# Graph layer with one-hot matmuls: two of the ten edge-against-slot comparison rows of a set made on ScalarE instead of VectorE

## The chip, the cores and the metric

The kernel runs on one core of a Trainium2 chip. The metric is the device time of one launch in microseconds. The time given for a kernel is the median of several runs; the profile shows one execution, whose own time is given beside its span.

## The reference

A graph has N = 6250 nodes with D = 64 features and E = 206250 edges, sorted by destination. What is computed is

```python
h   = relu(layernorm(x))                                # (6250, 64), no gain, no shift
msg = relu(h[src] + edge_attr)                          # (206250, 64)
agg = segment_sum(msg, dst, num_segments=6250)
out = x + relu((h + agg) @ W1 + b1) @ W2 + b2           # (6250, 64)
```

`dst` is sorted in ascending order; `src` is in no order, so `h[src]` is a gather.

## The kernel before, in words

**Groups and sets.** Edges are handled in groups of 1024 (128 partitions by 8 columns): 201 full groups and a short one at the end. Two groups, an even and an odd one, make a set `k`. Sets 2 to 99 take part in the scheme that the change touches: 98 sets.

**Two ways of fetching `h[src]`.** Of the 16 columns of a set, 10 are fetched by indirect DMAs on GpSimd's queue (`gather`, L160, one instruction for one column). The other 6 columns (4 of the even group and 2 of the odd one, `T = 6`) are fetched by TensorE with one-hot matrices, in three steps:

- Each edge of the six columns was given, in a ranking stage at the beginning, one of 128 slots in one of `SB = 10` parts of the nodes. For each set, `source` (L346) brings the node number of every slot into a row in DRAM and back, spread over all partitions. `find` (L365) compares that row with node numbers on VectorE, which gives `found`, and `slots_of` (L381) multiplies `found` with the table `hp` of h (three bf16 pieces that add up to the float32 value). The result is a PSUM tile `rows`, which ScalarE copies into the SBUF tile `picked` (`slots_out`, L393, L394). This is done for two parts at a time: 5 products of 10 matmuls and 5 copies for each set.
- `spot` (L359) loads a row of numbers that says in which part and slot each of the set's 768 edges lies, spread over all partitions. `back` (L373) compares this row with `ids`, the numbers 4096 + 128 m + partition, for each part m: ten comparisons of 768 elements for each set, 16-bit integers in and bf16 ones and zeros out. Their result is the one-hot matrix `backs`, slots by edges.
- `pick` (L406) multiplies `backs` with `picked`, ten matmuls for each of the six columns, into PSUM tiles `pick`. VectorE adds up the three pieces and the edge's attributes (L466).

**Messages and sums.** `messages` (L459) adds the gathered columns (L464, VectorE), reduces the `pick` tiles (L466, VectorE), and makes the ReLU on ScalarE (L469). `window_sum` (L472) sums messages into 48 destinations by matmuls with a one-hot matrix (L478). `take` (L450, L456) and `room` (L396, L403) copy edge attributes into PSUM on ScalarE ahead of time. Every 16 or 17 groups a finished block of 512 nodes goes through the two matrix products (`hidden`, `result`, `store`).

**Order.** The order of work is written out by hand: each engine works through its instructions in the order in which the Python code emits them. `half(g)` (L526) emits one group's part. For a set in the steady state the orders of the two engines that matter are:

- TensorE, even half: rows of parts 0 and 1; `source` products (L351); `window_sum` of the group before; rows of parts 2 and 3; `pick` of the odd group (20 matmuls). Odd half: rows of parts 4 and 5, of 6 and 7, of 8 and 9; `window_sum`; `pick` of the next even group (40 matmuls).
- ScalarE, even half: the `source` copy (L353); `picked` of parts 0 and 1; ReLU; `take`; `room`; `picked` of parts 2 and 3. Here `back` is called, after `pick`. Odd half: `picked` of parts 4 and 5, of 6 and 7; ReLU; `take`; `picked` of parts 8 and 9; `room` (two copies).

The PSUM tile `rows` has two buffers, used in turn by all of `slots_of` and `source`. So a product of `slots_of` can begin only when the tile two before it has been copied out by ScalarE:

```python
ps = psum.tile([P, 2, 3 * D], F32, name="rows", bufs=2)      # slots_of, L383
ps = psum.tile([SB, P], F32, name="rows", bufs=2)            # source, L349
```

`backs` and `spots` have two buffers each. Gathered columns have nine (`LOOK`), so GpSimd's gathers can run up to nine groups ahead of the messages.

Of the kernel before, what the change touches and what calls it, by code (L numbers as in the profile page):

```python
# [9 lines left out]
F32 = mybir.dt.float32  # L10
# [4 lines left out]
AF = mybir.ActivationFunctionType  # L15
# [5 lines left out]
P = 128  # L21
# [23 lines left out]
SB, BB, BN = 10, 5, 125  # L45
KB = SB * BB
PART = BB * BN
EVEN, ODD = 4, 2
T = EVEN + ODD
K0, K1 = 2, NG // 2  # L50
KS = K1 - K0
ROUND = 1.5 * 2 ** 23
# [8 lines left out]
def kernel(  # L61
# [14 lines left out]
    nc = tc.nc  # L76
    ctx.enter_context(tc.manual_schedule())

    const = ctx.enter_context(tc.tile_pool(name="const", bufs=1))
# [27 lines left out]
    for t_sb, tail in ((src_sb, src_tail), (dst_sb, dst_tail)):  # L107
# [18 lines left out]
    ones = const.tile([P, P], F32, name="ones")  # L126
# [11 lines left out]
    ids = const.tile([P, SB], F32, name="ids")  # L138
    nc.gpsimd.iota(ids, pattern=[[P, SB]], base=BIAS, channel_multiplier=1,
                   allow_small_or_imprecise_dtypes=True)  # L140
    hp = const.tile([P, KB, 3, D], BF16, name="hp")
    nc.vector.memset(hp[:, KB - 1], 0.0)

# [80 lines left out]

    part = const.tile([P, KS, T], BF16, name="part")
    node = const.tile([P, KS, T], F16, name="node")
    nodes_of = const.tile([P, BB], F32, name="nodes_of")
    nc.gpsimd.iota(nodes_of, pattern=[[P, BB]], base=1, channel_multiplier=1, allow_small_or_imprecise_dtypes=True)
    place = const.tile([P, KS, T], F32, name="place")
    spot_rows = dram.tile([KS * T, P], BF16, name="spot_rows")  # L230
    of_part = const.tile([P, SB], BF16, name="of_part")
    nc.gpsimd.iota(of_part, pattern=[[1, SB]], base=0, channel_multiplier=0, allow_small_or_imprecise_dtypes=True)
    fits = const.tile([P, KS, T], F32, name="fits")

    def of_sets(t_sb, even):
        v = t_sb[:, K0 * 2 * G:K1 * 2 * G].rearrange("p (k j) -> p k j", j=2 * G)
        return v[:, :, G - EVEN:G] if even else v[:, :, 2 * G - ODD:]
# [6 lines left out]
    def ranks(pool):  # L244
        src_f = pool.tile([P, KS, T], F32, name="src_f")
        nc.vector.tensor_copy(src_f[:, :, :EVEN], of_sets(src_sb, True))
# [81 lines left out]
    holds, masks, backs, sources, spots, found, picked, halves = {}, {}, {}, {}, {}, {}, {}, {}  # L328
# [44 lines left out]
    def back(k):  # L373

        row = spots.pop(k).bitcast(I16)
        backs[k] = hot.tile([P, SB, T, P], BF16, name="backs")
        for m in range(SB):
            nc.vector.tensor_scalar(backs[k][:, m].rearrange("p t s -> p (t s)"), row, ids[:, m:m + 1], None,  # L378
                                    op0=ALU.is_equal)

    def slots_of(k, m, n):  # L381

        ps = psum.tile([P, 2, 3 * D], F32, name="rows", bufs=2)  # L383
        for i in range(n):
            for b in range(BB):
                nc.tensor.matmul(ps[:, i], found[k][:BN, b, m + i, :],  # L386
                                 hp[:BN, (m + i) * BB + b].rearrange("p t d -> p (t d)"),
                                 start=(b == 0), stop=(b == BB - 1))
        if m == 0:
            picked[k] = hot.tile([P, SB, 3 * D], BF16, name="picked")  # L390
        halves[k, m] = ps[:, :n]
# [134 lines left out]
    def half(g, groups=True, sets=True):  # L526
# [36 lines left out]
        if even:  # L563
            if now:
                back(k + 1)
            if sets and is_set(k + 3):
                mask(k + 3)
        elif sets:
            if is_set(k + 2):
                find(k + 2)  # L570
            if is_set(k + 3):
                hold(k + 3)
# [43 lines left out]
    with tc.tile_pool(name="nodes", bufs=2) as nodes:  # L616

        for k, n in ((0, KB // 2), (KB // 2, KB - 1 - KB // 2), (KB - 1, 1)):
            p = min(BN, N - k * BN)
# [111 lines left out]
```

## Time and profile before

| | |
|---|---|
| time, median of 3 runs | 1386.8 us (1383.34 to 1388.13) |
| the profiled execution's own time | 1385.12 us |
| its span | 1383.3 us |
| mean granted TensorE clock | 0.964 of full speed |
| busy: TensorE matmul / weight load | 1242.3 us (90%) / 1163.1 us (84%) |
| busy: VectorE | 1185.2 us (86%) |
| busy: ScalarE | 508.4 us (37%) |
| busy: GpSimd | 1022.5 us (74%) |
| the ten comparisons of `back`, L378 | 980 instructions, 335.5 us, mean 415 ns |
| gathers, L160 (from `h_rows`) | 992 instructions, 987.2 us, mean 995 ns |

The span is the time from the first to the last instruction of the profiled execution. Engine shares are averages over the whole span. PE is TensorE's matmuls, PEld its weight loads, DVE is VectorE, ACT ScalarE, POOL GpSimd, and SP the engine that issues most DMAs. A line of the timeline gives the start in microseconds, the busy time, the engine, the line of the kernel, the operation with its output and input, the number of instructions merged into it, and in brackets the idle time before it and what ended it. Instructions of one engine can overlap by a tenth of a microsecond in the records.

### The profile page before, as it was taken

Reading aid. Unit: us, or ns where it says so; the run is one execution under the profiler, and the core shown is the slowest. Engines: PE = TensorE matmul, PEld = TensorE weight load, DVE = VectorE, ACT = ScalarE, POOL = GpSimd, SP = SyncE. Lnnn points to the kernel's source line nnn. Section 1 sums busy time; section 2 is a strip of 40 time slices with the busy share of each in tenths; the row PEclk is TensorE's granted clock in tenths of the full one; section 3 lists DMA queues with packets and bytes.
Section 4 is the critical chain, followed back from the end, with each engine's and each line's share of the span. In section 5 each row is a group of like instructions: output and inputs, shape, how many; then the busy total and the mean of one; then the engine's idle time right before and its main releaser. Section 6 shows DMA issues by size and latency. Waiting matters only on the chain.

```text
span 1383.3 us, 37550 instructions
## 1 busy us (share of the span) xinstructions
PE 1242.3 (90%) x14894; PEld 1163.1 (84%) x14894; DVE 1185.2 (86%) x2847; ACT 508.4 (37%) x1356; POOL 1022.5 (74%) x1035
## 2 busy tenths in 40 slices
PE   1624899999999999999999999999999999989994
PEld 0413799999999999999999999999998998988983
DVE  6765999899899899999898899898998998888972
ACT  2321333433343333443433433334333443333331
POOL 7672777777777777777777777777777777777774
PEclk9766999999999999999999999999999999999996
DMA  5331434434444444444444444444444443443431
GB/s 169 92 71 55 116 86 119 120 100 114 126 118 112 104 116 122 122 117 106 112 117 122 122 108 110 114 119 117 107 112 119 122 118 96 118 119 92 121 75 25
DMA packets 107766, 150.42 MB, mean 109 GB/s; under 512 B 33857, under 2 KB 52673, under 8 KB 107585
## 3 DMA queue, kind: packets, MB, share of 16 engines
q1 hardware_dynamic: 73569, 112.65, 27.5%
q0 software_dynamic: 32768, 33.62, 12.5%
q8 instruction: 118, 1.93, 0.6%
q10 hardware_dynamic: 1248, 1.70, 0.4%
q14 instruction: 63, 0.52, 0.1%
HBM read 144.27 MB, written 3.60 MB: 107 GB/s over the span
## 4 chain that ended last, share of the span: by engine, by line
PE 61%; DMA 8%; POOL 8%; DVE 6%; issue 5%; ACT 2%; DVEq 0%; POOLq 0%; SPq 0%; ACTq 0%
PE pick L412 27%; PE rows L386 21%; PE agg L478 10%; POOL xg L160 8%; DMA xg<-h_rows,src_sb 5%; PE rows L351 2%; DVE backs L378 2%; DVE full L466 1%; DVE found L370 1%; DMA sources<-source_row 1%; PE rows L499 1%; ACT picked L394 1%; PE rows L486 1%; DMA spots<-spot_rows 1%; ACT full L456 1%
## 5 line engine op out<-in xcount | busy, mean ns | idle before, releaser
L160 POOL DMA_INDIRECT xg<-h_rows,src_sb x992 | 987.2, 995 | 334.4 <-issue 264.3
L412 PE MATMUL pick<-picked,backs 128*128 128x192 bf16 x5880 | 517.1, 246 | 23.5 <-ACT pick L403 20.7
L412 PEld LDWEIGHTS <-backs 128*128 128x128 bf16 x5880 | 488.9, 98 | 28.2 <-issue 21.4
L386 PE MATMUL rows<-hp,found 125*128 125x192 bf16 x4900 | 459.8, 247 | 6.5 <-DVE found L370 5.7
L386 PEld LDWEIGHTS <-found 125*128 125x128 bf16 x4900 | 404.8, 98 | 18.3 <-DVE found L370 7.4
L378 DVE TENSOR_SCALAR backs<-spots,ids 128x768 bf16<-128x768 int16 x980 | 335.5, 415 | 0.0
L394 ACT CAST picked<-rows 128x384 bf16<-128x384 f32 x490 | 234.3, 478 | 274.2 <-PE rows L386 269.4
L370 DVE TENSOR_SCALAR found<-sources,nodes_of 125x1280 bf16<-125x1280 int16 x490 | 251.0, 577 | 38.0 <-DMA sources<-source_row 37.6
L466 DVE TENSOR_REDUCE full<-pick 128x128 f32<-128x512 f32 x294 | 205.7, 700 | 67.5 <-PE pick L412 36.0
L478 PEld LDWEIGHTS agg<-oh,msg 128*64 128x64 f32 x3224 | 205.7, 139 | 37.2 <-issue 19.4
L478 PE MATMUL agg<-oh,msg 128*64 128x48 f32 x3224 | 231.0, 226 | 4.3 <-ACT msg L469 4.3
L353 ACT CAST source<-rows 10x128 int16<-10x128 f32 x98 | 25.0, 255 | 456.4 <-PE rows L351 451.8
L469 ACT ACTIVATE msg<-full 128x512 f32<-128x512 f32 x202 | 119.5, 592 | 49.0 <-DVE full L466 26.8
L464 DVE TENSOR_TENSOR full<-full,xg 128x256 f32<-128x256 f32 (+1 forms) x202 | 99.1, 491 | 33.4 <-DMA xg<-h_rows,src_sb 22.8
L440 DVE TENSOR_TENSOR oh<-slot,wslots 128x384 f32<-128x384 int16 x202 | 109.9, 544 | 0.0
L333 DVE TENSOR_TENSOR holds<-place,wslots 128x768 f16<-128x768 f32 x98 | 92.4, 943 | 6.0 <-DMA spot_rows<-sp 6.0
L456 ACT COPY full<-ea 128x256 f32<-128x256 f32 (+1 forms) x202 | 87.2, 432 | 0.0
L403 ACT COPY pick<-ea 128x128 f32<-128x128 f32 x294 | 72.0, 275 | 0.0
L351 PE MATMUL rows<-holds,mask 128*10 128x128 f16 x588 | 49.6, 221 | 4.6 <-DVE mask L343 4.6
L351 PEld LDWEIGHTS <-mask 128*10 128x10 f16 x588 | 31.5, 88 | 21.7 <-issue 19.9
L435 DVE TENSOR_TENSOR z<-z,agg 64x48 f32 x202 | 38.2, 189 | 6.4 <-PE agg L478 3.3
L160 POOL DMA_INDIRECT xg<-in_x_dram,src_sb x32 | 33.4, 1044 | 10.9 <-issue 9.4
(101 smaller groups left out, 284.4 us busy)
## 6 DMA issues: line engine op xcount, KB each, us to landing
ea<-in_edge_attr_dram SPq DMA_DIRECT2D x201, 256.0 KB
sources<-source_row SPq DMA_DIRECT2D x98, 320.0 KB
spots<-spot_rows SPq DMA_DIRECT2D x98, 192.0 KB
xg<-h_rows,src_sb POOLq DMA_INDIRECT x992
source_row<-source SPq DMA_DIRECT2D x98, 2.5 KB
x_sb<-in_x_dram SPq DMA_DIRECT2D x4, 384.0 KB
h_rows<-ln_h SPq DMA_DIRECT2D x4, 384.0 KB
xb<-in_x_dram SPq DMA_DIRECT2D x12, 128.0 KB
```

Source lines behind the costliest of these rows:

```text
L160: nc.gpsimd.indirect_dma_start(out=xg[:, j, :], out_offset=None, in_=rows[:, :], in_offset=bass.IndirectOffsetOnAxis(ap=idx[:, j:j + 1], a ...
L351: nc.tensor.matmul(ps, mk[:, t, :], oh[:, t, :], start=(t == 0), stop=(t == T - 1))
L370: nc.vector.tensor_scalar(found[k][:BN, b].rearrange("p m s -> p (m s)"), row[:BN], nodes_of[:BN, b:b + 1], None, op0=ALU.is_equal)
L378: nc.vector.tensor_scalar(backs[k][:, m].rearrange("p t s -> p (t s)"), row, ids[:, m:m + 1], None, op0=ALU.is_equal)
L386: nc.tensor.matmul(ps[:, i], found[k][:BN, b, m + i, :], hp[:BN, (m + i) * BB + b].rearrange("p t d -> p (t d)"), start=(b == 0), stop=(b ...
L394: nc.scalar.copy(picked[k][:, m:m + n], halves.pop((k, m)))
L412: nc.tensor.matmul(pk[:, u, :3].rearrange("p t d -> p (t d)"), backs[k][:, m, t0 + i + u, :], picked[k][:, m], start=(m == 0), stop=(m == ...
L440: nc.vector.tensor_tensor(oh[:, :n], slot[:, cols_of(g)].unsqueeze(2).to_broadcast([P, n, W]), wslots[:, :W].unsqueeze(1).to_broadcast([P, ...
L456: nc.scalar.copy(full[:, :n], taken[g][2][:, :n])
L466: nc.vector.tensor_reduce(full[:, m + i:m + i + c], pk[:, :c].rearrange("p j t d -> p j d t"), AX.X, ALU.add)
L469: nc.scalar.activation(msg[:, :n], full[:, :n], AF.Relu)
L478: nc.tensor.matmul(pa, msg[:, j, :], oh[:, j, :], start=(j == 0), stop=(j == n - 1))
```

## The change

A constant `ids_neg` is made once, the negative of `ids`. In `back`, VectorE makes the comparisons for parts 0 to 7. For parts 8 and 9 ScalarE makes two activations each: the absolute value of the edge's number less the slot's number, written as bf16, and then in place the ReLU of one less that distance, which is 1 where the numbers agree and 0 elsewhere. ScalarE's instructions are emitted where `back` is called, that is behind the copy of `picked` for parts 2 and 3.

```diff
+SA = 2
...
+    ids_neg = const.tile([P, SB], F32, name="ids_neg")
+    nc.vector.tensor_scalar_mul(ids_neg, ids, -1.0)
...
         row = spots.pop(k).bitcast(I16)
         backs[k] = hot.tile([P, SB, T, P], BF16, name="backs")
-        for m in range(SB):
+        for m in range(SB - SA):
             nc.vector.tensor_scalar(backs[k][:, m].rearrange("p t s -> p (t s)"), row, ids[:, m:m + 1], None,
                                     op0=ALU.is_equal)
+        for m in range(SB - SA, SB):
+            at = backs[k][:, m].rearrange("p t s -> p (t s)")
+            nc.scalar.activation(at, row, AF.Abs, bias=ids_neg[:, m:m + 1])
+            nc.scalar.activation(at, at, AF.Relu, bias=ones[:, 0:1], scale=-1.0)
```

## The prediction, made before the changed kernel was run

> **What bounds the kernel now.** I read the page's busy shares and its chain first, then the timeline of TensorE and of ScalarE over one set, then the groups by shape for durations, and the waits.
>
> ```profile
> PE 1242.3 (90%) x14894; PEld 1163.1 (84%) x14894; DVE 1185.2 (86%) x2847; ACT 508.4 (37%) x1356; POOL 1022.5 (74%) x1035
> ...
> PE 61%; DMA 8%; POOL 8%; DVE 6%; issue 5%; ACT 2%; DVEq 0%; POOLq 0%; SPq 0%; ACTq 0%
> ```
>
> ScalarE is busy for only 37% and hardly appears in the chain, while TensorE carries 61% of it. That makes ScalarE look free. Whether it is free at the moment when the new work arrives is a question for the timeline. TensorE, one set:
>
> ```profile
> 711.13 0.99 PE L386 MATMUL rows<-hp,found 125*128 125x192 bf16 x10
> 712.05 0.50 PE L351 MATMUL rows<-holds,mask 128*10 128x128 f16 x6
> 712.48 1.13 PE L478 MATMUL agg<-oh,msg 128*64 128x48 f32 x16
> 713.54 1.00 PE L386 MATMUL rows<-hp,found 125*128 125x192 bf16 x10
> 714.38 1.81 PE L412 MATMUL pick<-picked,backs 128*128 128x192 bf16 x20
> 716.03 2.64 PE L386 MATMUL rows<-hp,found 125*128 125x192 bf16 x30
> 718.60 1.13 PE L478 MATMUL agg<-oh,msg 128*64 128x48 f32 x16
> 719.76 3.46 PE L412 MATMUL pick<-picked,backs 128*128 128x192 bf16 x40
> 723.06 0.99 PE L386 MATMUL rows<-hp,found 125*128 125x192 bf16 x10
> ```
>
> The set repeats after 723.06 - 711.13 = 11.93 us, and no line shows idle time in front: here TensorE is the bound, and whatever holds it back lengthens the set. The starts of L353, one for each set, show the same 11.93 us in over half of the 97 distances. ScalarE in the same set:
>
> ```profile
> 714.58 0.48 ACT L394 CAST picked<-rows 128x384 bf16<-128x384 f32 x1 [0.31 <-PE rows L386]
> 717.05 0.48 ACT L394 CAST picked<-rows 128x384 bf16<-128x384 f32 x1 [2.00 <-PE rows L386]
> 717.88 0.48 ACT L394 CAST picked<-rows 128x384 bf16<-128x384 f32 x1 [0.34 <-PE rows L386]
> 718.26 0.60 ACT L469 ACTIVATE msg<-full 128x512 f32<-128x512 f32 x1
> 718.75 0.39 ACT L456 COPY full<-ea 128x256 f32<-128x256 f32 x1
> 719.05 0.49 ACT L394 CAST picked<-rows 128x384 bf16<-128x384 f32 x1
> 719.42 0.48 ACT L403 COPY pick<-ea 128x128 f32<-128x128 f32 x2
> 724.51 0.26 ACT L353 CAST source<-rows 10x128 int16<-10x128 f32 x1 [4.61 <-PE rows L351]
> ```
>
> ScalarE's idle time lies in two pieces: 2.00 us before the copy of parts 4 and 5, and 4.61 us at the end of the set. `back` is called between the first and the second line shown, so the new work falls into the piece of 2.00 us.
>
> GpSimd is the second bound. Its gathers take 995 ns each with 0.30 us between them, some 1.29 us from start to start (310 gathers from 700 to 1100 us), so 12.9 us for the ten of a set: more than 11.93. It starts with a lead of up to nine groups and loses it. The waits show "DVE full L464 <- DMA xg" with 22.8 us, all of it after 1000 us.
>
> **What one activation costs.** No activation in the trace reads 16-bit integers, so I go by the nearest shapes:
>
> ```profile
> L191 ACT ACTIVATE ln_sq<-ln_xc 128x768 f32<-128x768 f32 x4 | 3.3, 838 | 22.9 <-DMA w_sb<-in_w_dram 13.1 <-DVE ln_xc L189 9.9
> ...
> L197 ACT ACTIVATE ln_v<-ln_v,eps_sb 128x12 f32<-128x12 f32 x4 | 1.2, 304 | 0.8 <-DVE ln_v L196 0.8
> ...
> L105 ACT ACTIVATE warm<-eps_sb 128x1 f32<-128x1 f32 x1 | 0.2, 203 | 0.0
> ```
>
> 768 elements take 838 ns without a bias from SBUF. L197 has such a bias and takes 304 ns for 12 elements, L105 has none and takes 203 ns for one: the bias costs some 92 ns. So 0.93 us for each new activation. Independent neighbours start 0.10 us before the end of the one ahead (L394 lasts 0.48 us, its successor starts after 0.38). A dependent one can't: on VectorE L343 reads what L340 has written and starts 0.03 us after its end. So Abs to ReLU is 0.96 us, ReLU to the next 0.83, and the four take X = 2 x 0.96 + 2 x 0.83 = 3.58 us from start to start. Bounds: 4 x (0.838 - 0.10) = 2.95 us without the bias price and with every overlap; 4 x 0.96 = 3.84 us with none. I take 3.58, since L197's bias and L343's dependency are the nearest rows to what the change issues.
>
> The Trainium skill, "ScalarE: Activation LUTs", section "What ACT_TABLE_LOAD costs", gives 280 ns + 0.833 ns an element with a bias pointer, an estimate of 0.92 us here, and the same rate for bf16 as for fp32. The trace's 128-element bf16 copy (L639, 267 ns) against the fp32 one (L403, mean 275 ns) also shows no gain for 16 bits; no row shows int16.
>
> **The step on the path.** ScalarE is free at 714.58 + 0.38 = 714.96. The new work holds it until 714.96 + 3.58 = 718.54; only then comes the copy of parts 4 and 5, which now starts at 717.05. It ends at 719.02. Behind it in ScalarE's queue are the copy of parts 6 and 7, the ReLU, `take`, the copy of 8 and 9 and `room`. The product of parts 8 and 9 is what waits first: it needs the `rows` buffer of parts 4 and 5. It starts now at 716.03 + 2 x 0.83 = 717.69, and the copy ended at 717.53, so there is 0.11 us of slack when 0.05 is allowed for the signal. New start 719.07: delay D = X - 2.20 = 1.38 us.
>
> Does it grow? ScalarE goes on at 718.92, 719.30, 719.79, 720.09 and 720.46 (`room`, whose first copy ends by 720.75). TensorE does parts 8 and 9 to 719.90 and the window sum to about 721.0, and then `pick`, for which `room` is just in time. Nothing is added, and nothing is won back in the rest of the set, since TensorE has no idle time there. ScalarE's 4.61 us at the end absorb its own lateness, so that the next set begins undisturbed: each set costs D once.
>
> **The rest of the change.** VectorE loses 2 x 0.345 us for each set (ten comparisons in 3.45 us from 700.20 us). It ends no wait of TensorE in the set shown, so this is worth nothing by itself. `pick` reads rows 8 and 9 at about 721.1; they are ready at 718.6. `spots` is released by the second Abs at about 717.6 rather than at 715.3 us; SP's queue holds the next `spots` load until then, and the attribute loads behind it, but `spots` is used two sets later, the attributes six groups later, and SP's next urgent job, the `source` row, comes after 724 us: no cost while these 7 us last. `ids_neg` is one small operation at the start, beside waits for `x`: nothing.
>
> **What comes back.** The 95 distances from the third L353 (138.6 us) to the last (1328.0) sum to 1189.4 us. Of these 95 x 11.93 = 1133.4 are regular; 28.0 are the eleven finished blocks (six sets with 14.40, five pairs of 13.11 and 13.38); 8.1 is one set of 20.06 us with the single `find_left`, whose VectorE work would cover one D; 19.7 are irregular, most of them late gathers. With 11.93 + 1.38 + 0.3 (blocks) = 13.6 us a set, TensorE is slower than GpSimd's 12.9, gathers keep their lead, and the 19.7 go. So do the waits for the last gathers behind the sets: VectorE waits 4.57 us at 1356.1, 8.08 at 1366.1 and 3.44 at 1370.8, of which some 10 us end the time, the rest being covered by other work.
>
> **Sum**, from the profiled execution's own 1385.1 us: + 95 x 1.38 = 131.1; + 2.8 for the two sets after the last L353; - 1.4 for the covered one; - 19.7; - 10: 1488. The median stands 1.7 us above that execution: 1490 us. With X = 2.95 (D = 0.75) the same sum gives 1428 + 2 = 1430; with X = 3.84 (D = 1.64) 1513 + 2 = 1515, and if half of the 29.7 us stay, 1530.
>
> **Rivals.** *It fits into the gap.* If ScalarE handled 16-bit data at about twice the rate, X would be at most 2.20 us, 0.55 us for each activation with its overlap; D is nil and the result is not slower. VectorE's 0.69 us could then shorten some of the irregular 19.7 us, but gathers would still be the limit late in the run: 1370 to 1387 us. L639 and L403 speak against it, and L191's rate of 838 ns for 768.
>
> *Table loads.* The trace has one ACT_TABLE_LOAD of 1283 ns (L105) for Sqrt, Square, ReLU and copies; Abs isn't among them. Were it in another set than those, each set of edges would need four loads: X = 3.58 + 4 x 1.28 = 8.7, D = 6.5, and 1385 + 97 x 6.5 - 36 = about 1980 us. Against it: one load served all four functions used so far. The skill's same page, section "Table sets: the hidden batching unit", says that relu, copy and abs are in every set: by that no load is added, and the sum stays at 1490. No run here shows Abs yet.
>
> *The clock falls.* Gaps of 1.4 us in every set could lower the granted clock. For it: 120 to 150 us had 0.81 at 81% busy. At that clock the 11.65 us of matmuls become 14.4, which adds 2.7 us a set: about 1750. Against it: at 1323.27 us TensorE had been idle for 2.27 us, and the next 40 matmuls took 3.46 us, as everywhere.
>
> **Numbers.** Forecast 88%, fit 5%, table loads 3%, clock 4%. About 0.3% (4 us) is what a measurement can tell from no change; the fit lies beyond it in some two of its five. The range of 1435 to 1530 takes in the bounds of X, with the last few microseconds at the low end left out.
>
> **What would show it.** Right: four activations a set of about 0.93 us behind the L394 copy; the third L386 product of the odd half starting 1.4 us later, its wait put down to ACT L394; sets of 13.3 us; waits for xg gone; no second table load; clock 1.0 in the middle. Wrong: activations of 0.5 us, no idle time of TensorE before L386, or sets still of 11.93 us.

## The result, and the profile after

The changed kernel takes 1483.35 us (median of 4 runs, 1481.2 to 1485.22), the kernel before 1385.93 us beside it. The ratio is 1.0707, with a 95% interval of 1.0693 to 1.0721: 7% slower. The profiled execution took 1483.27 us, with a span of 1481.4 us. The forecast was 1490 us.

From the page of the changed kernel, the busy shares and the chain by engine:

```profile
PE 1253.2 (85%) x14894; PEld 1160.5 (78%) x14894; DVE 1129.0 (76%) x2652; ACT 830.4 (56%) x1748; POOL 1016.7 (69%) x1035
...
PE 60%; ACT 30%; DVE 4%; issue 3%; DMA 2%; SPq 0%; DVEq 0%; ACTq 0%
```

ScalarE's share of the chain goes from 2% to 30%, at a busy share of only 56%. The timeline of ScalarE, one set, shows where:

```profile
760.70 0.48 ACT L401 CAST picked<-rows 128x384 bf16<-128x384 f32 x1 [0.32 <-PE rows L393]
761.07 0.94 ACT L385 ACTIVATE backs<-spots,ids_neg 128x768 bf16<-128x768 int16 x1
762.04 0.94 ACT L386 ACTIVATE backs<-backs,ones 128x768 bf16<-128x768 bf16 x1
762.89 0.92 ACT L385 ACTIVATE backs<-spots,ids_neg 128x768 bf16<-128x768 int16 x1
763.84 0.94 ACT L386 ACTIVATE backs<-backs,ones 128x768 bf16<-128x768 bf16 x1
764.68 0.84 ACT L401 CAST picked<-rows 128x384 bf16<-128x384 f32 x2
765.41 0.61 ACT L476 ACTIVATE msg<-full 128x512 f32<-128x512 f32 x1
765.90 0.39 ACT L463 COPY full<-ea 128x256 f32<-128x256 f32 x1
766.21 0.49 ACT L401 CAST picked<-rows 128x384 bf16<-128x384 f32 x1
766.59 0.47 ACT L410 COPY pick<-ea 128x128 f32<-128x128 f32 x2
771.94 0.26 ACT L356 CAST source<-rows 10x128 int16<-10x128 f32 x1 [4.88 <-PE rows L354]
```

The idle piece of 2.00 us in front of the copy of parts 4 and 5 has gone, and the copies of parts 4 to 7 follow the activations without a gap (`x2`). The 4.61 us at the end have become 4.88. TensorE in the same set:

```profile
757.25 0.99 PE L393 MATMUL rows<-hp,found 125*128 125x192 bf16 x10
758.17 0.50 PE L354 MATMUL rows<-holds,mask 128*10 128x128 f16 x6
758.60 1.13 PE L485 MATMUL agg<-oh,msg 128*64 128x48 f32 x16
759.66 1.00 PE L393 MATMUL rows<-hp,found 125*128 125x192 bf16 x10
760.50 1.82 PE L419 MATMUL pick<-picked,backs 128*128 128x192 bf16 x20
762.15 1.81 PE L393 MATMUL rows<-hp,found 125*128 125x192 bf16 x20
765.19 0.99 PE L393 MATMUL rows<-hp,found 125*128 125x192 bf16 x10 [1.22 <-ACT picked L401]
766.10 1.13 PE L485 MATMUL agg<-oh,msg 128*64 128x48 f32 x16
767.17 3.47 PE L419 MATMUL pick<-picked,backs 128*128 128x192 bf16 x40
770.48 0.99 PE L393 MATMUL rows<-hp,found 125*128 125x192 bf16 x10
```

The 30 matmuls that ran through before are split into 20 and 10, and the last ten wait for the copy of `picked`. The set takes 770.48 - 757.25 = 13.23 us, 1.30 more than before. In the list of waits it is

```profile
PE rows L393 <- ACT picked L401: 106.3, 86, 2.3
```

that is 86 times, 106.3 us in total, the longest 2.3 us. The other sets have a finished block's product in this place, which waits instead.

### The profile page after: what moved, and what is told of

The parts are those of the page before. It is cut to its first block, busy times and chain, and to the rows that moved or that the text cites. A ratio compares the mean times of both kernels' runs of the same rounds, so it can differ in the third digit from the quotient of the medians.

```text
span 1481.4 us, 37674 instructions
## 1 busy us (share of the span) xinstructions
PE 1253.2 (85%) x14894; PEld 1160.5 (78%) x14894; DVE 1129.0 (76%) x2652; ACT 830.4 (56%) x1748; POOL 1016.7 (69%) x1035
## 4 chain that ended last, share of the span: by engine, by line
PE 60%; ACT 30%; DVE 4%; issue 3%; DMA 2%; SPq 0%; DVEq 0%; ACTq 0%
PE pick L419 23%; PE rows L393 18%; PE agg L485 14%; ACT backs L386 12%; ACT backs L385 11%; ACT picked L401 6%; PE rows L354 3%; PE rows L506 1%; PE rows L493 1%; DMA ea<-in_edge_attr_dram 1%; DMA x_sb<-in_x_dram 1%; DVE where L279 0%; ACT z L222 0%; DVE here L278 0%; DMA spot_rows<-sp 0%
## 5 line engine op out<-in xcount | busy, mean ns | idle before, releaser
L393 PE MATMUL rows<-hp,found 125*128 125x192 bf16 x4900 | 475.2, 248 | 112.8 <-ACT picked L401 106.3
L419 PEld LDWEIGHTS <-backs 128*128 128x128 bf16 x5880 | 484.0, 98 | 8.0 <-issue 1.0
L356 ACT CAST source<-rows 10x128 int16<-10x128 f32 x98 | 24.9, 254 | 481.3 <-PE rows L354 481.3
L381 DVE TENSOR_SCALAR backs<-spots,ids 128x768 bf16<-128x768 int16 x784 | 272.8, 418 | 0.0
L401 ACT CAST picked<-rows 128x384 bf16<-128x384 f32 x490 | 222.2, 473 | 45.7 <-PE rows L393 45.7
L485 PEld LDWEIGHTS agg<-oh,msg 128*64 128x64 f32 x3224 | 205.9, 139 | 33.4 <-issue 15.5
L386 ACT ACTIVATE backs<-backs,ones 128x768 bf16<-128x768 bf16 x196 | 183.2, 935 | 6.4
L385 ACT ACTIVATE backs<-spots,ids_neg 128x768 bf16<-128x768 int16 x196 | 182.0, 928 | 0.0
```

What stands on the lines that cost most here:

```text
L385: nc.scalar.activation(at, row, AF.Abs, bias=ids_neg[:, m:m + 1])
L386: nc.scalar.activation(at, at, AF.Relu, bias=ones[:, 0:1], scale=-1.0)
L393: nc.tensor.matmul(ps[:, i], found[k][:BN, b, m + i, :], hp[:BN, (m + i) * BB + b].rearrange("p t d -> p (t d)"), start=(b == 0), stop=(b ...
L401: nc.scalar.copy(picked[k][:, m:m + n], halves.pop((k, m)))
L419: nc.tensor.matmul(pk[:, u, :3].rearrange("p t d -> p (t d)"), backs[k][:, m, t0 + i + u, :], picked[k][:, m], start=(m == 0), stop=(m == ...
L485: nc.tensor.matmul(pa, msg[:, j, :], oh[:, j, :], start=(j == 0), stop=(j == n - 1))
```

## The experiments

The theory: what costs is not the amount of ScalarE's work but its place in ScalarE's queue. The four activations stand in front of a copy that TensorE needs soon, in an idle piece that holds about half of them. The rivals: a cost for each activation, wherever it stands; a cost of handing rows of `backs` to a second engine; VectorE's relief as part of the sum.

Four kernels were first run on a chip on which the kernel before took 2043.47 us (median of 23 runs). In a set of the one-row kernel's trace from there, ScalarE's `source` copy began 2.28 us after the end of the products that it reads (717.56 to 719.84 us), where it takes 0.03 us in the kernel before, and the traces don't show why. Their ratios (1.0027 for one row, 1.0747 for three, 1.0118 for the late place, 0.9999 for VectorE's relief alone) can't be compared with the rest, and their expectations in microseconds failed with the base. All four kernels were run again where the kernel before takes 1385 to 1387 us; those runs decide.

### One row instead of two

```diff
-SA = 2
+SA = 1
```

First try (1.0027 [0.9985, 1.0069], on the chip named above):

> ScalarE makes one row instead of two (SA = 1), at the same place in its queue. Theory (the place: only what exceeds the idle piece of 2.00 us in front of the copy of parts 4 and 5 costs; with the measured set of 13.23 us the delay is X - 2.31 us): X = 0.96 + 0.84 = 1.80 us is below 2.31, so the delay is nil, sets of 11.93 us, 1386 us within 5. Rival (the cost goes with the number of activations): half of the 97 us, about 1435 us. Rival (any hand-over of rows of backs to a second engine costs, whatever its length): 1435 to 1483 us.

Again:

> The kernel of one_row, once more where the kernel before takes 1386 us and not 2043 us. Theory (the place: only what exceeds the idle piece of 2.00 us in front of the copy of parts 4 and 5 costs; delay X - 2.31 us): X = 0.96 + 0.84 = 1.80 us, delay nil, sets of 11.93 us, 1386 us within 5. Rival (cost in proportion to the number of activations): about 1435 us.

Measured: 1384.19 us, ratio to the kernel before 0.9988 [0.9976, 1.0000]. Timeline of ScalarE:

```profile
715.81 0.48 ACT L401 CAST picked<-rows 128x384 bf16<-128x384 f32 x1 [0.31 <-PE rows L393]
716.19 0.94 ACT L385 ACTIVATE backs<-spots,ids_neg 128x768 bf16<-128x768 int16 x1
717.16 0.94 ACT L386 ACTIVATE backs<-backs,ones 128x768 bf16<-128x768 bf16 x1
718.29 0.48 ACT L401 CAST picked<-rows 128x384 bf16<-128x384 f32 x1 [0.20 <-PE rows L393]
```

One row fits: of the 2.00 us of idle time 0.20 are left, and the sets are 11.93 us again. Half of the work costs nothing, not half of 97 us, and a second engine that writes `backs` costs nothing either. Both rivals fall.

### Three rows

```diff
-SA = 2
+SA = 3
```

First try (1.0747 [1.0647, 1.0847], on the chip named above):

> ScalarE makes three rows (SA = 3), at the same place. Theory of the place: X = 3 x 1.80 = 5.41 us, delay 5.41 - 2.31 = 3.10 us, sets of 15.03 us, 1483 + 97 x 1.80 = 1658 us within 8. Rival (cost in proportion to the number of activations): 1386 + 1.5 x 97 = 1532 us.

Again:

> The kernel of three_rows (three rows on ScalarE, at the place of the change), once more where the kernel before takes 1386 us. Theory of the place: X = 3 x 1.80 = 5.41 us, delay 5.41 - 2.31 = 3.10 us, sets of 15.03 us, 1483 + 97 x 1.80 = 1658 us within 8. Rival (cost in proportion to the number of activations): 1386 + 1.5 x 97 = 1532 us.

Measured: 1779.5 us, ratio 1.2848 [1.2814, 1.2883]. That is far above the proportional rival and also 121 us above the theory. TensorE's timeline shows both parts:

```profile
713.00 1.82 PE L393 MATMUL rows<-hp,found 125*128 125x192 bf16 x20
717.83 1.38 PE L393 MATMUL rows<-hp,found 125*128 125x192 bf16 x10 [3.02 <-ACT picked L401]
719.14 1.95 PE L485 MATMUL agg<-oh,msg 128*64 128x48 f32 x16
721.02 3.78 PE L419 MATMUL pick<-picked,backs 128*128 128x192 bf16 x40
```

The wait is 3.02 us, as the theory has it. But the matmuls behind it are slower: 1.38 us for ten instead of 0.99, 1.95 for the sums instead of 1.13, 3.78 for `pick` instead of 3.47. Of the 95 distances of L356 from the third to the last, 22 are the 15.02 us of the theory and 56 lie between 16.53 and 16.62; the other 17 hold finished blocks or `find_left`. The mean granted clock is 0.897, against 0.967 with two rows: it is 0.50 for 3.41 us at a time, as from 701.20 to 704.61 and again from 718.27 to 721.68 us. The 95 distances sum to 1580.96 us, 118 more than 95 x 15.03 and the 35.3 us that blocks and `find_left` cost in the changed kernel; that is nearly all of the missing 121 us. So the theory had the wait right and left out what the wait does to the clock. Here the prediction's rival of the falling clock appears, with a gap of 3.02 us in every set; with 1.22 us in every set it doesn't.

### The same four activations in the other idle piece

ScalarE's part of `back` is emitted at the end of the odd half, behind `room`, for the set after; VectorE's part stays where it was.

```diff
+    def back_act(k):
+        row = spots[k].bitcast(I16)
+        backs[k] = hot.tile([P, SB, T, P], BF16, name="backs")
+        for m in range(SB - SA, SB):
+            ...                                  # Abs and Relu as in the change
     def back(k):
         row = spots.pop(k).bitcast(I16)
-        backs[k] = hot.tile([P, SB, T, P], BF16, name="backs")
         ...
             if is_set(k + 3):
                 hold(k + 3)
+            if is_set(k + 2):
+                back_act(k + 2)
```

First try (1.0118 [1.0046, 1.0190], on the chip named above):

> The same four activations for each set, but emitted at the end of the odd half, behind the two copies of room, one set half ahead of VectorE's eight comparisons, where ScalarE has 4.61 us of idle time. Theory of the place: 3.61 us fit, sets of 11.93 us again, waits for late gathers back, 1386 us within 6 (a few us below if VectorE's relief helps the gathers). Rival (the amount of work on ScalarE, or its use of memory beside the other engines, is what costs): about 1480 us as with the change.

Again:

> The kernel of late (four activations behind the two copies of room, in ScalarE's idle piece of 4.61 us), once more where the kernel before takes 1386 us. Theory of the place: sets of 11.93 us, 1386 us within 6. Rival (the amount of work on ScalarE, or its use of memory beside other engines): about 1480 us.

Measured: 1379.86 us, ratio 0.9950 [0.9935, 0.9965]. ScalarE's timeline:

```profile
717.73 0.48 ACT L413 COPY pick<-ea 128x128 f32<-128x128 f32 x2
718.12 0.95 ACT L381 ACTIVATE backs<-spots,ids_neg 128x768 bf16<-128x768 int16 x1
719.10 0.94 ACT L382 ACTIVATE backs<-backs,ones 128x768 bf16<-128x768 bf16 x1
719.95 0.92 ACT L381 ACTIVATE backs<-spots,ids_neg 128x768 bf16<-128x768 int16 x1
720.90 0.94 ACT L382 ACTIVATE backs<-backs,ones 128x768 bf16<-128x768 bf16 x1
722.82 0.26 ACT L356 CAST source<-rows 10x128 int16<-10x128 f32 x1 [0.99 <-PE rows L354]
```

The same work, each instruction as long as in the change, costs nothing here; 0.99 us of idle time are left, and the sets are 11.93 us. This is the test that separates place from amount, and it goes to the place. The kernel is even 0.5% faster than the one before.

### Three buffers for `rows`

```diff
-    wslots = psum.tile([P, P], F32, name="wslots", bufs=1)
-    nc.vector.tensor_copy(wslots, slots[:, :P])
+    wslots = slots[:, :P]
 ...
-    psum.tile(..., name="rows", bufs=2)
+    psum.tile(..., name="rows", bufs=3)          # in all places
```

> The change with three buffers for the PSUM tile rows instead of two; to make room in PSUM the constant wslots lies in SBUF. Theory: the product of parts 8 and 9 no longer waits for the copy of parts 4 and 5, and the next thing that is late is room's first copy, behind all of it in ScalarE's queue: in the changed kernel it ends 753.36 + 0.27 = 753.63, and pick would be due at 748.92 + 3.73 = 752.65, so a delay of 1.02 us is left of 1.30: sets of 12.95 us, 1483 - 97 x 0.28 = 1456 us within 8, and TensorE waits for ACT pick instead of ACT picked. Rival (the two buffers are the only way in which ScalarE's lateness reaches TensorE): 1386 us. Rival (the buffers have nothing to do with it): 1483 us.

Measured: 1440.33 us, ratio 1.0404 [1.0383, 1.0425]; sets of 12.97 us. TensorE:

```profile
716.43 1.13 PE L484 MATMUL agg<-oh,msg 128*64 128x48 f32 x16
718.63 3.46 PE L418 MATMUL pick<-picked,backs 128*128 128x192 bf16 x40 [1.06 <-ACT pick L409]
```

As expected, the wait has moved from the third product to `pick`, which waits 1.06 us for `room`'s copy: the two buffers set where ScalarE's lateness is met first, and with more of them it is met one step later, 0.26 us smaller. The total is 16 us below the expectation for a reason beside the theory: the eleven finished blocks cost 15.5 us (six sets of 14.24, five pairs of 13.51 and 14.00, each less 12.97) instead of 28, since their products use `rows` too, and the first sets cost 4 us less. The move of `wslots` also makes the gathers longer (last section); in the sets shown TensorE waits for `room` alone.

### ScalarE's work without VectorE's relief

```diff
-        for m in range(SB - SA):
+        for m in list(range(SB - SA)) + list(range(SA)):
             nc.vector.tensor_scalar(...)
```

> The change, with VectorE making ten comparisons again (after parts 0 to 7 it repeats those of parts 0 and 1), so that only ScalarE's added work is left of the change. Theory: VectorE's relief is worth nothing inside the set, 1483 us within 4, sets of 13.23 us. Rival (the relief is worth its 0.69 us a set, and the change would have cost 165 us without it): about 1550 us.

Measured: 1486.72 us, ratio 1.0736 [1.0714, 1.0757], sets of 13.23 us. That is 3 us above the change, and the intervals of the two ratios overlap (1.0714 to 1.0757 here, 1.0693 to 1.0721 for the change): inside the change VectorE's relief is worth a few microseconds at most, not the 67 us of the rival.

### VectorE's relief without ScalarE's work

```diff
-                    nc.tensor.matmul(..., backs[k][:, m, t0 + i + u, :],
+                    nc.tensor.matmul(..., backs[k][:, m, t0 + i + u, :] if m < SB - SA else none,
```

The four activations are left out as well; `none` is a tile of zeros, so the matmuls for parts 8 and 9 still run but add nothing.

First try (0.9999 [0.9957, 1.0041], on the chip named above):

> VectorE makes eight comparisons and nobody makes the other two; pick's matmuls for parts 8 and 9 run with a constant tile of zeros as weights, so the edges whose source lies in parts 8 and 9 get no gathered value in the six columns. Theory: VectorE ends no wait in a set, so its 0.69 us are worth nothing there: sets of 11.93 us, 1378 to 1387 us, what is gained being only fewer late gathers. Rival (VectorE's time counts and the change gave it back elsewhere): 1386 - 97 x 0.69 = 1319 us.

Again:

> The kernel of relief (VectorE makes eight comparisons, nobody the other two; pick's matmuls for parts 8 and 9 run with zeros as weights, so edges whose source lies there get no gathered value in the six columns), once more where the kernel before takes 1386 us. Theory: sets stay at 11.93 us, and the time is that of late, which does the same work for VectorE with ScalarE's activations in its idle time: 1380 us within 3. Rival (ScalarE's activations cost late something that VectorE's relief pays for): 1370 us or less.

Measured: 1381.4 us, ratio 0.9967 [0.9953, 0.9980]. The sets stay at 11.93 us, and the time is within 2 us of the late place, 1379.86: at that place ScalarE's part is free, and the gain over the kernel before is VectorE's relief.

### Three rows in both idle pieces, and three in the late one

One row at the place of the change and two at the place of `late`:

> Three rows on ScalarE, one at the place of the change (1.80 us, below 2.31) and two at the place of late (3.61 us, below 4.61); VectorE makes seven comparisons. Theory of the places: no delay, sets of 11.93 us, 1378 us within 4, with the gathers the only thing left to gain. Rival (three rows cost because they are three): some 1430 us or more, on the way to the 1779 us of three_rows_again.

Measured: 1378.56 us, ratio 0.9936 [0.9923, 0.9949], the lowest of all, though its interval overlaps that of the late place (0.9935 to 0.9965). Three rows cost 394 us in one place and nothing when spread over two.

All three at the late place:

> Three rows on ScalarE, all at the place of late. Theory of the places: late left 0.99 us idle in front of the source copy, and one more row takes 1.80, so the next set's copies start 0.81 us late; room's copy for the odd group, with some 0.07 us of slack, passes it on to pick: a delay of 0.74 us, sets of 12.67 us. 1380 + 97 x 0.74 = 1452 us, less some 24 us of waits for gathers that go: 1428 us within 10, with TensorE waiting for ACT pick. Rival (in the long idle piece nothing is urgent, three rows are as free as two): 1380 us.

Measured: 1416.39 us, ratio 1.0206 [1.0188, 1.0224], 2 us below the range given. The sets are 12.56 us, not 12.67:

```profile
727.62 1.81 PE L422 MATMUL pick<-picked,backs 128*128 128x192 bf16 x20 [0.44 <-ACT pick L413]
```

The wait is where the theory put it, at the next set's `pick`, but the delay is 0.63 us instead of 0.74. The expectation took the `source` copy to start 1.80 - 0.99 = 0.81 us late. Counted from the start of TensorE's set it starts 0.71 us late (2.17 us behind 723.74, against 1.46 behind 721.36 in the late kernel), since it begins 0.10 us before the end of the last activation (725.91, where that ends at 726.01): the 0.99 us of idle time had room for that much more. The late idle piece has an end too.

## Why the prediction was right

**The cost of an activation.** Right. 0.93 us and X = 3.58 us for four were forecast from L191, L197, L105 and the dependent pair on VectorE. Measured, in the groups of the changed kernel by shape:

```profile
L386 ACT ACTIVATE backs<-backs,ones 128x768 bf16<-128x768 bf16 x196 | 183.2, 935 | 6.4
L385 ACT ACTIVATE backs<-spots,ids_neg 128x768 bf16<-128x768 int16 x196 | 182.0, 928 | 0.0
```

and X = 764.68 - 761.07 = 3.61 us. The estimate of 0.92 us from the Trainium skill, "ScalarE: Activation LUTs", section "What ACT_TABLE_LOAD costs", agrees. That section gives one rate for fp32 and bf16; here 16-bit integers are read no faster either (928 ns against 935 ns with bf16), which ended the rival of the fit. The trace has one table load of 1283 ns, at the start, as before: no second one, as the section "Table sets: the hidden batching unit" has it for Abs.

**The place and the wait.** Right: third product of the odd half, put down to ACT `picked`. One row below the bound, two and three above it, and the late place agree with the rule that only what exceeds the idle piece, and the slack behind it, costs, and the third buffer shows the way through `rows`.

**The size of D.** 1.38 us were forecast, 1.30 measured. The step that failed is "nothing is won back in the rest of the set". The third product did start 1.38 us later (3.04 us behind the start of the 20, where the 30 matmuls before began their last ten after 2 x 0.83 = 1.66). But `pick`, which before began 1.16 us after the window sum (718.60 to 719.76), begins 1.07 us after it now (766.10 to 767.17): before, `room`'s first copy (719.42, some 0.27 us long) had ended only just ahead of it, and now it ends 0.3 us ahead. So the window sum to `pick` gives back 0.09 us in each set; 95 x 0.08 = 8 us of the sum.

**What comes back.** Right for the waits: the 95 distances between the third and the last source copy sum to 1292.2 us; less 95 x 13.23 = 1256.9, 27.9 of finished blocks and 7.4 of the `find_left` set (20.64 us), nothing is left of the 19.7 irregular us. VectorE's waits for gathered columns, 22.8 us before, are 0.2 us. The part behind the last source copy shrank from 55.3 to 45.9 us, by 9.4, where the sum had 10 - 2.8 = 7.2.

**The beginning.** Not in the sum: the third source copy comes at 143.28 instead of 138.62 us, 4.7 us later. In the first set TensorE waited 2.33 us for `picked`. The granted clock had been 1.00 from 130.5 to 133.8 us; behind the wait, from 133.9 to 140.7 us, it was 0.50, and the 40 matmuls of the first `pick` took 5.48 us instead of 3.46. So the rival of the falling clock, given 4% for every set, appeared in this one, which the sum leaves out:

```profile
134.01 1.76 PE L393 MATMUL rows<-hp,found 125*128 125x192 bf16 x10 [2.33 <-ACT picked L401]
136.51 5.48 PE L419 MATMUL pick<-picked,backs 128*128 128x192 bf16 x40 [0.74 <-ACT pick L410]
```

**The sum.** 95 x 1.30 = 123.5, less 19.7 and 0.7 (`find_left`), plus 4.7, less 9.4: 98.4, against 1481.4 - 1383.3 = 98.1 us. The forecast had 102.8 for the same execution. A start that the sum leaves out (4.7) and an overestimated D (8) partly cancel, so some of the closeness of 1490 to 1483.35 us is luck.

**VectorE's relief.** "Worth nothing by itself" holds inside the set and in the change. It was slightly wrong in general: where nothing else is late, it is worth 4 to 9 us (two rows alone, two and three rows at free places), and the last gather starts earlier by about as much (below).

## What to carry to other kernels

An engine that is busy for 37% isn't free for 37% of the time at any place: look in its timeline for the idle piece into which the new instruction will fall, and for the first instruction behind it that another engine needs. Work up to the length of that piece costs nothing. What goes beyond it, less the slack of the instructions that wait, is paid once for each round: here 3.61 us of work met an idle piece of 2.00 us and cost 1.30 us a set. It can cost more where the gap lowers the clock, as with three rows. The same four instructions cost 97 us at one place of the queue and nothing half a set earlier. When an in-order engine helps another, choose the place first and the amount by the gap.

## What the runs showed of the hardware

**The granted clock and gaps.** A gap of 1.22 us in every set left the clock at 1.00 in the stretch from 300 to 1100 us. A gap of 3.02 us in every set lowered it behind most gaps (56 sets of 16.53 to 16.62 us against 22 of 15.02), most often to 0.50 for 3.41 us. The Trainium skill, "TensorE: Matmul & The Clock Gate", section "What's actually happening", has the clock fall after an idle window of about 3.4 us. The three-row kernel differs in that gaps of 3.02 us were enough in most sets. The length of a gap alone doesn't decide it in these traces. The clock fell behind the 2.33 us in the changed kernel's first set, but not behind 2.27 and 2.52 us in the kernel before (the `pick` products at 1323.27 and 1258.76 us took 3.46 us). With three rows at the late place it fell to 0.50 for 3.41 us twice, from 572.28 and from 1319.80 us, in sets with a finished block whose longest gap was 1.05 us. What else decides was not tested.

**VectorE and the gathers.** Where sets take 11.93 us, the mean gather gets shorter with fewer comparisons on VectorE: 995 ns with ten, 992 with nine (one row), 990 and 991 with eight (late, and VectorE's relief alone), 989 with seven (three rows in both pieces). The steps are small: kernels with the same number of comparisons differ by as much (991 ns with ten where the change has VectorE's relief taken away, 989 with eight in the change). Inside the changed kernel's trace, 231 gathers run beside comparisons of `backs` for more than 0.3 us and take 1004 ns in the mean; the 725 that meet none take 984. The last gather starts at 1368.3, 1366.4, 1364.9, 1362.7 and 1362.0 us (before, one row, late, relief, three rows in both pieces), and the same executions took 1385.12, 1383.33, 1381.9, 1379.46 and 1378.69 us, each 16.7 to 17.0 us more: the time follows the last gather. That shorter gathers are what makes it start earlier is likely but not tested by itself. In the other direction, the kernel with three `rows` buffers, whose `wslots` VectorE reads from SBUF rather than PSUM, has gathers of 1035 ns:

```profile
L162 POOL DMA_INDIRECT xg<-h_rows,src_sb x992 | 1027.1, 1035 | 335.3 <-issue 262.9
```

against 989 ns in the changed kernel with two buffers. Two things differ there, the buffers and `wslots`; which of them it is can be read from the overlaps. The 95 gathers that run beside `holds<-place,slots` (L335), one of the comparisons that read `wslots`, for more than 0.3 us take 1381 ns in the mean, and the 829 that meet none 993. In the changed kernel, where `wslots` lies in PSUM, it is 951 ns for 91 gathers and 985 for 840. So the gathers lengthen beside the comparisons that read `wslots` from SBUF. That gathers and VectorE stand in each other's way is measured; by what mechanism is not. The Trainium skill, "SBUF — State Buffer", section "Who interferes with whom", says that GpSimd and VectorE share a pair of SBUF ports, that some forms of `tensor_scalar` take the pair, and that an operation with two SBUF inputs takes its read side; both measurements agree with this in direction.
